# Layer 0 of an image network: the rows of cumulated steps from one transpose in place of four products with the triangle

## The chip, the core and the metric

The kernel runs on one core of a Trainium2 chip. The metric is the device time of one execution in microseconds (us); the number given for a kernel is the median of several runs. The engines are named as in the profile: PE is TensorE (matrix products), PEld its weight loads, DVE VectorE, ACT ScalarE, POOL GpSimd, SP SyncE, which here issues the DMAs.

## The reference, cut to what matters

Eight images of 64x64 pixels with 192 channels go through two layers. Layer 0 is, for each image: a group normalization, a 3x3 depthwise convolution, a layer norm, an input projection, a causal convolution of four taps, a state-space mixer (SSD) with 6 heads of 64 channels and 64 states, a gate and an RMS norm, an output projection, another 3x3 convolution, a layer norm and an MLP. Layer 1 is a selective scan in four directions. The change touches only the mixer of layer 0. What it computes there:

```python
dt = softplus(zxbcdt[..., DIN + CONVDIM:] + dt_bias)      # a step for each token and head
dA = dt * A                                               # A = -exp(A_log), one for each head
dA_cs = cumsum(dA, axis=2)                                # cumulated inside a chunk of tokens
seg = dA_cs[:, :, :, None, :] - dA_cs[:, :, None, :, :]   # token i minus token j, for each head
scores = einsum('bcin,bcjn->bcij', Cm, Bm)[..., None] * exp(seg) * dt[:, :, None, :, :]   # where j <= i
y = einsum('bcijh,bcjhp->bcihp', scores, x)
decay_last = exp(dA_cs[:, :, -1:, :] - dA_cs)
```

For `seg` the cumulated steps are needed twice: with the tokens along the partitions (as columns, one number for each partition), and with the tokens along the free axis (as rows), repeated on every partition.

## The kernel before, in words

Layer 0 (`layer0`) works on 64 tiles: 8 images times 8 tiles of 512 tokens (TT), each tile in 4 chunks (NQ) of 128 tokens (Q). The work of a tile is written as some eighteen chains (`statistics`, `inputs`, `conv1`, `norm1`, `gate`, `mix`, `convolve`, `steps_in_time`, `decays`, `powers`, `scores`, `turn`, `states`, `mixer`, `output`, `conv2`, `norm2`, `mlp`), each a generator that runs over all tiles and yields steps. Chains of different tiles overlap.

The order of the work on each engine is set by a planner, `Flow`. A step names its engine, an estimated duration (in us), and the instructions to issue. The planner keeps a clock for each engine; it takes again and again the step that can begin earliest (with a small rank for each chain as a tie-break), issues its instructions, and moves the clocks. `yield "take", tag` takes a buffer from a small pool ("mm": five PSUM banks of 512 columns; "sm": three; "csr": one), `f.give` returns it with its time, and `f.at[...]` notes when a result is due, for the chains that wait for it. An ACT step may name a table; where it differs from the current one, the planner counts a table load. The order that comes out is the order in which each engine works through its queue on the chip; the engines meet by semaphores only. So an estimate that is changed can move any later step on any engine.

The steps around the change, with their lines:

- `gate` (L531) makes p_z: the gate and the raw steps dr of a tile. L547 (DVE) adds the bias to dr.
- `steps_in_time` makes dt (ACT L566 to L568, DVE L577) and da = dt x A (DVE L578, 128 tokens x 4 chunks x 6 heads), then on PE three products with da (L588): with a strictly lower triangle, with an upper triangle `up` (1 where column >= row), and with ones. They go to p_c, 24 columns each. The middle 24 columns are the cumulated steps as columns; DVE copies them to cst (L594). ACT takes the exponential of all 72 columns (dec, L601), and DVE makes w2 from it (L607).
- `rows_of`, forked from there, makes the same cumulated steps as rows: for each chunk one product of da (128 tokens x 6 heads, the weights) with `up` (128 x 128, streamed), into p_cs, 6 rows x 512 columns (L617). ACT copies them to csr (L622), and SP stores csr in a scratch tensor csd in HBM (L625), [6, 512].
- `decays` loads from csd, for each chunk, the six rows of 128 numbers onto all 128 partitions: e (L640), 128 x 6 x 128.
- `powers` (ACT L653, L658) makes exp(-(relu(cs_i - e))) in e; its bias is a column of cst. `scores` multiplies e with the masked product p_g (L673, L677, L682), and `mixer` uses e as the weights of p_y (L790), after the skip products (L787).
- Other steps that are named below: p_x (L448, input projection), p_t and xdt, xw (L699, L705, L710: transposes of x and their weighting), p_b and bt (L715, L720), p_i and p_n (L740, L751, states), p_u and yc (L850, L859), p_o (L873), p_f (L956 and L976, the two halves of the MLP), the convolution steps xs and x on DVE (L343), and the sums s on POOL (L365).

Layer 1 begins after layer 0 has ended, and works with other functions.

Of the kernel before, what the change touches and what calls it, by code (L numbers as in the profile page):

```python
# [8 lines left out]
F32 = mybir.dt.float32  # L9
# [8 lines left out]
TT = 512  # L18
RT = TT // WI
NT = L // TT  # L20
Q = 128
NQ = TT // Q
NH, HD, NS = 6, 64, 64
# [30 lines left out]
def bc(ap, axis, shape):  # L54

    return ap.unsqueeze(axis).to_broadcast(shape)
# [37 lines left out]
class Flow:  # L94
# [24 lines left out]
    def pool(self, tag, n):  # L119
        self.slots[tag] = [0.0] * n  # L120
# [64 lines left out]
def step(engine, weight, do, after=None, table=None):  # L185
    return engine, weight, do, after, table


def layer0(tc, consts, x, x1s, mv1, w_in, w_out, w_fc1, w_fc2, rows):
    nc = tc.nc  # L190
    ident, low, up, grp, eps, ones96, ones1, p96, p128 = consts
# [10 lines left out]
    with ExitStack() as ctx:  # L202
# [6 lines left out]
        sp = pool("s0", 2)  # L209
        xxp = pool("xx0", 3)  # L210
        mp = pool("mm0", 5, space=PSUM)
        dsp = pool("cs0", 3, space=DRAM)
# [11 lines left out]
        ps = mp.tile([128, TT], F32, name="p_fb", tag="mm")  # L224
        for mt in range(6):
            for ct in range(CT):
# [4 lines left out]
                    start=ct == 0,  # L231
                    stop=ct == 1,
# [22 lines left out]
        f = Flow(tc)  # L255
# [4 lines left out]
        got = {}  # L260
# [294 lines left out]
        def steps_in_time():  # L555

            for T in range(len(tiles)):
                yield "wait", ("dr", T)
                dr = got["dr", T]
                dt = got["dt", T] = sp.tile([128, NQ, NH], F32, name="dt")  # L560
                da = got["da", T] = sp.tile([128, NQ, NH], F32, name="da")
                yield step(
                    "ACT",
                    0.8,
                    lambda: [
                        nc.scalar.activation(dt, dr, AF.Abs),  # L566
                        nc.scalar.activation(dt, dt, AF.Exp, scale=-1.0),
                        nc.scalar.activation(dt, dt, AF.Ln, bias=1.0),  # L568
                    ],
                    None,  # L570
                    "explog",
                )
                yield step(
                    "DVE",
                    0.4,
                    lambda: [
                        nc.vector.scalar_tensor_tensor(dt, dr, 0.0, dt, ALU.max, ALU.add),  # L577
                        nc.vector.tensor_mul(da, dt, bc(an, 1, [128, NQ, NH])),  # L578
                    ],
                )  # L580
                daf = da.rearrange("p a b -> p (a b)")
                yield "take", "sm"
                pc = qp.tile([128, DIN], F32, name="p_c", tag="sm")
                r = yield step(
                    "PE",
                    0.8,
                    lambda: [
                        nc.tensor.matmul(pc[:, i * 24 : i * 24 + 24], m, daf, start=True, stop=True)  # L588
                        for i, m in enumerate((low, up, ones1))
                    ],  # L590
                )
                cst = got["cst", T] = sp.tile([128, NQ, NH], F32, name="cst")
                yield step(
                    "DVE", 0.16, lambda: [nc.vector.tensor_copy(cst.rearrange("p a b -> p (a b)"), pc[:, 24:48])], r  # L594
                )
                f.fork(rows_of(T, da))
                dec = got["dec", T] = sp.tile([128, 3, NQ, NH], F32, name="dec")
                r = yield step(
                    "ACT",
                    0.3,  # L600
                    lambda: [nc.scalar.activation(dec.rearrange("p a b c -> p (a b c)"), pc[:, 0:72], AF.Exp)],  # L601
                    r,
                    "explog",
                )
                f.give("sm", r)
                w2 = got["w2", T] = sp.tile([128, NQ, NH], F32, name="w2")
                f.at["w2", T] = yield step("DVE", 0.2, lambda: [nc.vector.tensor_mul(w2, dt, dec[:, 0])])  # L607

        def rows_of(T, da):

            yield "take", "mm"
            ps = mp.tile([128, TT], F32, name="p_cs", tag="mm")
            r = yield step(
                "PE",
                1.0,
                lambda: [
                    nc.tensor.matmul(ps[:NH, c * Q : c * Q + Q], da[:, c], up, start=True, stop=True) for c in range(NQ)  # L617
                ],
            )
            yield "take", "csr"  # L620
            csr = sp.tile([NH, TT], F32, name="csr", bufs=1)
            r = yield step("ACT", 0.6, lambda: [nc.scalar.copy(csr, ps[:NH])], r)  # L622
            f.give("mm", r)
            csd = got["csd", T] = dsp.tile([NH, TT], F32, name="csd")
            r = yield step("SP", 0.1, lambda: [nc.sync.dma_start(out=csd, in_=csr)], r)  # L625
            f.give("csr", r + 2)
            f.at["cs", T] = r + 2.5
# [4 lines left out]
        def decays():  # L632

            for T in range(len(tiles)):
                yield "wait", ("cs", T)
                for c in range(NQ):
                    yield "take", "e"
                    e = got["e", T, c] = ch.tile([128, NH, Q], F32, name="e", bufs=5)
                    src = got["csd", T][:, c * Q : c * Q + Q].partition_broadcast(128)
                    r = yield step("SP", 0.1, lambda: [nc.sync.dma_start(out=e, in_=src)], f.at["cs", T])  # L640
                    f.at["csb", T, c] = r + 3

# [366 lines left out]
        for gen, rank in (  # L1009
            (mlp, -0.177),  # L1010
            (norm2, -0.056),
            (conv2, -0.275),
            (output, -0.03),
            (mixer, -0.08),
            (states, -0.04),
            (turn, -0.06),
            (scores, 0.017),
            (powers, -0.284),
            (decays, -0.195),
            (steps_in_time, 0.209),  # L1020
            (convolve, 0.071),
            (mix, -0.12),
            (gate, -0.17),
            (norm1, -0.14),
            (conv1, -0.254),
            (inputs, -0.313),
            (statistics, -0.298),
        ):
            f.chain(gen(), rank)
# [864 lines left out]
```

## Time and profile before

| | |
|---|---|
| median of 3 runs | 23751.5 us (23744.67 to 23764.05) |
| the profiled execution: its own time | 23759.13 us |
| its span, from first to last instruction | 23757.4 us |
| layer 0 in it (end of the last MLP product) | 0 to 4868 us |
| granted TensorE clock, mean | 0.972 |
| p_cs L617, 64 tiles x 4 products | 512 matmul instructions |
| csr<-p_cs L622, ACT | 64 x 575 ns (median) |
| cst<-p_c L594, DVE | 64 x 172 ns (median) |
| csd<-csr L625, SP issue | 64 x 283 ns (median) |
| e<-csd L640, SP issue, 384 KB each | 256 x 494 ns (median) |
| ACT_TABLE_LOAD in layer 0 | 356, 456.7 us |

An f32 product is recorded as two matmul instructions, a transpose as one. Matmuls are pipelined, so their recorded durations overlap. PEclk is the share of full clock that TensorE was granted. A row of who waited for whom names the waiter, the releaser, the total in us, how often, and the longest wait. The chain of waits is followed back from the last instruction: at each step to what released it, or to the instruction before it on its engine.

### The profile page before, as it was taken

How to read it: one execution, taken by the hardware profiler on the slowest of the kernel's cores; microseconds unless marked ns; L12 is line 12 of the kernel's file. 1: busy time of each engine (PE TensorE's matmuls, PEld its weight loads, DVE VectorE, ACT ScalarE, POOL GpSimd, SP SyncE). 2: the span in 40 equal slices, each digit the busy share in tenths (PEclk: the TensorE clock that was granted, in tenths of full speed). 3: DMA queues.
4: the chain of work that ended last, by engine and by line, in shares of the span. 5: the costliest groups of instructions: out<-in, count | busy, mean ns of one | idle time of the engine just before them, and what ended most of it. 6: DMA issues, size and time to landing. Idle time of an engine off the chain costs nothing.

```text
span 23757.4 us, 313126 instructions
## 1 busy us (share of the span) xinstructions
PE 21089.6 (89%) x100804; PEld 10279.5 (43%) x100804; DVE 21274.2 (90%) x22093; ACT 21040.0 (89%) x37507; POOL 16067.4 (68%) x12871
## 2 busy tenths in 40 slices
PE   7999999978888888888888888888888888888888
PEld 4444444434444444444444444444444444444444
DVE  7888888779998999899989998999899989998998
ACT  5666766669998999899989998999899989998998
POOL 1111111149995999599959985998699769976997
PEclk8999999989999999999999999999999999999999
DMA  2111111133233323333233233323332233233332
GB/s 50 45 44 44 46 44 43 39 99 81 81 79 107 81 82 78 107 81 82 76 112 81 82 77 109 81 81 79 110 82 81 78 107 82 81 85 100 82 83 67
DMA packets 1368290, 1859.75 MB, mean 78 GB/s; under 512 B 268576, under 2 KB 697024, under 8 KB 1357440
## 3 DMA queue, kind: packets, MB, share of 16 engines
q1 hardware_dynamic: 1366656, 1839.73, 28.7%
q8 instruction: 810, 13.27, 0.2%
q14 instruction: 824, 6.75, 0.1%
HBM read 1225.98 MB, written 210.50 MB: 60 GB/s over the span
## 4 chain that ended last, share of the span: by engine, by line
POOL 43%; PE 24%; ACT 15%; DVE 7%; issue 6%; DMA 4%; SPq 1%; POOLq 0%; ACTq 0%; DVEq 0%
POOL hc L1648 40%; ACT pw L1592 6%; ACT ea L1607 6%; POOL cy L1646 3%; PE p_f L956 3%; DMA xc<-xo 2%; DVE xs L1202 2%; PE p_f L976 2%; PE p_x L448 2%; PE y L1663 2%; PE p_o L873 2%; PE p_y L790 1%; PE g L1618 1%; PE p_d L1481 1%; PE p_z L531 1%
## 5 line engine op out<-in xcount | busy, mean ns | idle before, releaser
L1648 POOL TENSOR_TENSOR hc<-hs,cb 128x1024 f32<-128x1024 f32 x6144 | 14592.9, 2375 | 12.0 <-POOL cy L1646 9.9
L1634 DVE TENSOR_TENSOR_SCAN hs<-ea,cy,g 128x512 f32<-128x512 f32 x10752 | 13024.0, 1262 | 608.6 <-PE g L1618 411.1
L1592 ACT ACTIVATE pw<-duT,bt 128x384 f32<-128x384 f32 x16384 | 8874.1, 601 | 20.2 <-DVE duT L1539 20.2
L1607 ACT ACTIVATE ea<-dr,an 128x512 f32<-128x512 f32 x12288 | 8120.5, 709 | 189.2 <-DVE hs L1634 170.8
L1663 PE MATMUL y<-hc,sel 128*64 128x512 f32 x24576 | 6624.0, 617 | 1841.3 <-POOL hc L1648 1819.2
L1618 PEld LDWEIGHTS g<-ident,pw 128*128 128x128 f32 x49152 | 5288.7, 141 | 4336.8 <-issue 2671.4
L1618 PE MATMUL g<-ident,pw 128*128 128x128 f32 x49152 | 6788.4, 279 | 60.1 <-ACT pw L1592 28.6
L1646 POOL COPY cy<-hs 128x2 f32<-128x2 f32 x6144 | 1164.2, 189 | 3373.5 <-DMA out_x<-xl 1733.8
L1663 PEld LDWEIGHTS y<-hc,sel 128*64 128x64 f32 x24576 | 1225.9, 134 | 3254.1 <-POOL hc L1648 3031.3
L1634 DVE TENSOR_TENSOR_SCAN hs<-ea,g 128x512 f32<-128x512 f32 x1536 | 1763.7, 1202 | 159.0 <-PE g L1618 115.6
L365 POOL TENSOR_TENSOR s<-xs 96x512 f32<-96x512 f32 x64 | 121.1, 1892 | 2033.7 <-DVE xs L343 1522.9
L1202 DVE SCALAR_TENSOR_TENSOR xs<-pad,p,xs 128x4096 f32<-128x4096 f32 x192 | 860.9, 4484 | 43.4 <-ACT xs L1192 36.2
L1510 PE MATMUL p_dt<-xdbl,wd 13*128 13x512 f32 x1536 | 857.2, 639 | 41.0 <-DVE de L1523 39.1
L365 POOL TENSOR_TENSOR s<-sq 96x512 f32<-96x512 f32 x128 | 211.6, 1653 | 964.1 <-ACT sq L378 899.8
L1481 PE MATMUL p_d<-xc,wx 128*44 128x512 f32 x1536 | 791.6, 598 | 22.6 <-DMA xc<-xo 22.0
L343 DVE SCALAR_TENSOR_TENSOR x<-xx,p,x 96x512 f32<-96x512 f32 x1024 | 785.2, 815 | 19.4 <-ACT x L332 19.4
L956 PE MATMUL p_f<-h,wf 96*128 96x512 f32 x1536 | 761.9, 632 | 24.4 <-ACT zs L550 14.0
L343 DVE SCALAR_TENSOR_TENSOR xs<-xin,p,xs 96x512 f32<-96x512 f32 x1024 | 749.3, 767 | 4.6 <-ACT xs L332 4.6
L976 PE MATMUL p_f<-m,wf 128*96 128x512 f32 x1536 | 692.9, 601 | 0.0
L1532 PEld LDWEIGHTS p_du<-ident,de 128*128 128x128 f32 x3072 | 323.5, 141 | 610.2 <-DVE de L1523 405.8
L448 PE MATMUL p_x<-h,wi 96*128 96x512 f32 x1024 | 544.5, 664 | 12.3 <-ACT h L405 11.1
L365 POOL TENSOR_TENSOR s<-x 96x512 f32<-96x512 f32 x64 | 96.2, 1502 | 626.3 <-DVE x L343 477.2
(202 smaller groups left out, 19557.2 us busy)
## 6 DMA issues: line engine op xcount, KB each, us to landing
cb<-cd SPq DMA_DIRECT2D x4096, 128.0 KB
dr<-de SPq DMA_DIRECT2D x3072, 128.0 KB
xc<-xo SPq DMA_DIRECT2D x256, 768.0 KB
e<-csd SPq DMA_DIRECT2D x256, 384.0 KB
xl<-x SPq DMA_DIRECT2D x256, 384.0 KB
ut<-xo SPq DMA_DIRECT2D x128, 768.0 KB
ut<-xo SPq DMA_DIRECT2D x256, 384.0 KB
xo<-xs SPq DMA_DIRECT2D x48, 1024.0 KB
```

Of the source, the lines that this page charges most:

```text
L343: nc.vector.scalar_tensor_tensor(im(out[:, ct]), tap(ct, j), w[:, ct, j : j + 1], im(out[:, ct]), ALU.mult, ALU.add)
L956: nc.tensor.matmul(ps, wf1[:, ct, mt * 128 : mt * 128 + 128], h[:, ct], start=ct == 0, stop=ct == 1)
L976: nc.tensor.matmul(ps[:CP], wf2[:, kt, ct * CP : ct * CP + CP], m[:, kt], start=kt == 0, stop=kt == 5)
L1202: nc.vector.scalar_tensor_tensor(xs, tap(j), kw[:, d, j : j + 1], xs, ALU.mult, ALU.add)
L1481: nc.tensor.matmul(st["p_d"][:44], wx[:, d, k], st["xc"][:, d], start=d == 0, stop=d == DT - 1)
L1592: nc.scalar.activation(st["pw", p, j][:, :, i], st["duT"][:, j].rearrange("p (g c) -> p g c", c=64), AF.Copy, scale=st["bt"][:, j, n : n + 1],
L1607: nc.scalar.activation(ea[:, f], state[s]["dr", d][:, f], AF.Exp, scale=an[:, k, p, at : at + 1])
L1618: nc.tensor.transpose(g[:, f, j * 128 : j * 128 + 128], state[s]["pw", p, j][:, 2 * d + f].rearrange("p a b -> p (a b)"), ident,)
L1634: nc.vector.tensor_tensor_scan(rev(h[:, f]), rev(ea[:, f]), rev(g[:, f]), 0.0 if first(s) else state[s - 1]["cy"][:, p, d, f : f + 1], ALU ...
L1646: o(nc.gpsimd.tensor_copy(st["cy"][:, p, d], h[:, :, last]))
L1648: o(nc.gpsimd.tensor_mul(hc, h, bc(st["cb", p], 1, [128, 2, TT])))
L1663: o(nc.tensor.matmul(y[half[f]], sel, hc[:, f], start=p == 0 and k > 0, stop=p == NP1 - 1))
```

## The change

`rows_of` no longer multiplies da with the triangle. It takes cst, the cumulated steps as columns (128 tokens x 24: 4 chunks x 6 heads), and transposes it on PE: 24 rows x 128 columns, a row for each chunk and head. The copy csr, the scratch tensor csd and the loads of e follow the new layout: csr and csd are [24, 128], and chunk c's six rows lie at c x 6. The step on PE is now ready when cst is (q), and its estimate is 0.2 in place of 1.0; the estimate of ACT's copy is 0.3 in place of 0.6.

```diff
                 cst = got["cst", T] = sp.tile([128, NQ, NH], F32, name="cst")
-                yield step(
+                q = yield step(
                     "DVE", 0.16, lambda: [nc.vector.tensor_copy(cst.rearrange("p a b -> p (a b)"), pc[:, 24:48])], r
                 )
-                f.fork(rows_of(T, da))
+                f.fork(rows_of(T, cst, q))
...
-        def rows_of(T, da):
+        def rows_of(T, cst, r):
 
             yield "take", "mm"
             ps = mp.tile([128, TT], F32, name="p_cs", tag="mm")
             r = yield step(
                 "PE",
-                1.0,
-                lambda: [
-                    nc.tensor.matmul(ps[:NH, c * Q : c * Q + Q], da[:, c], up, start=True, stop=True) for c in range(NQ)
-                ],
+                0.2,
+                lambda: [nc.tensor.transpose(ps[: NQ * NH, :Q], cst.rearrange("p a b -> p (a b)"), ident)],
+                r,
             )
             yield "take", "csr"
-            csr = sp.tile([NH, TT], F32, name="csr", bufs=1)
-            r = yield step("ACT", 0.6, lambda: [nc.scalar.copy(csr, ps[:NH])], r)
+            csr = sp.tile([NQ * NH, Q], F32, name="csr", bufs=1)
+            r = yield step("ACT", 0.3, lambda: [nc.scalar.copy(csr, ps[: NQ * NH, :Q])], r)
             f.give("mm", r)
-            csd = got["csd", T] = dsp.tile([NH, TT], F32, name="csd")
+            csd = got["csd", T] = dsp.tile([NQ * NH, Q], F32, name="csd")
             r = yield step("SP", 0.1, lambda: [nc.sync.dma_start(out=csd, in_=csr)], r)
...
-                    src = got["csd", T][:, c * Q : c * Q + Q].partition_broadcast(128)
+                    src = got["csd", T][c * NH : c * NH + NH].partition_broadcast(128)
```

## The prediction

> **What bounds the kernel now.** I read the busy table in two stretches first, layer 0 (0 to 4868 us, where the last product of its MLP ends) and the rest, because every changed line stands in layer 0.
>
> ```profile
> core 0: us, PE busy (x) PEld busy (x) DVE busy (x) ACT busy (x) POOL busy (x), PEclk, DMA share, GB/s
> 0.00:4868.00 4868.00, 4496.60 (x15272) 2235.76 (x15272) 3899.60 (x6459) 3178.97 (x6133) 704.51 (x548) 0.92 0.18 44
> 4868.00:23757.00 18889.00, 16593.03 (x85533) 8043.76 (x85532) 17374.60 (x15634) 17861.01 (x31374) 15362.92 (x12323) 0.99 0.32 87
> ```
>
> In layer 0 PE is busy 92% of the time, DVE 80%, ACT 65%; the granted clock is 0.92. Next, who waits for whom between 100 and 4650 us (waiter, releaser, us in total, times, longest): PE's largest rows, then DVE's largest.
>
> ```profile
> PE p_c L588 <- DVE da L578: 42.6, 19, 4.8
> PE p_b L715 <- DVE xw L710: 27.2, 34, 2.4
> PE p_u L850 <- ACT yt L843: 24.7, 21, 4.4
> ...
> DVE xdt L705 <- PE p_y L790: 353.8, 142, 8.7
> ```
>
> PE's waits are small and spread; DVE waits for PE far more than PE for DVE. PE's idle time from 100 to 4750 us is 294 of 4650 us, 4.6 us for each of the 64 tiles. Then the chain of waits, asked in stretches of 150 us over layer 0: I added its pieces by engine and got PE 3792 us, DVE 800, ACT 197, DMA 57. So PE's in-order queue sets the pace, with DVE taking over for about a sixth. One stretch shows the products in question:
>
> ```profile
> 1574.90 1.11 PE p_c L588 x6
> 1576.01 1.47 PE p_n L751 x2
> 1577.48 3.71 PE p_f L956 x4
> 1581.19 1.80 PE p_cs L617 x8
> ```
>
> The columns are start, length, engine, tile and line, and how many instructions; x8 is four products of two instructions each.
>
> Last, the tile p_cs itself (min/median/max ns):
>
> ```profile
> L617 PEld LDWEIGHTS p_cs<-up,da x512: 83/88/136, 84.6 to 4662.7; 128*6 128x6 f32 x171
> L617 PE MATMUL p_cs<-up,da x512: 272/273/421, 84.6 to 4662.8; 128*6 128x128 f32 x171
> L622 ACT COPY csr<-p_cs x64: 558/575/577, 89.0 to 4663.6; 6x512 f32<-6x512 f32 x64
> ```
>
> Its 273 ns is not its cost, since products overlap. I therefore took each of the 64 groups in the trace from its first matmul's start to the start of the next group on PE: 41 of them take 0.97 us, 16 take 1.80, the others from 1.15 to 5.74; the mean is 1.33 and the sum 84.9 us. On the chain of waits lie 40 of the 64, with 49.4 us.
>
> **What the Trainium skill says.** "TensorE: Matmul & The Clock Gate", Part 4 (PE-mode transpose): about 275 ns for a 128x128 transpose in a kernel, output to PSUM, so that a copy must follow. The trace agrees in the duration (p_t at L699: median 273 ns), but in a stream three p_t take 0.33 us, so a step is 0.11 us. Same page, Part 1: the array runs at half clock after an idle window. The trace agrees: p_cs takes 0.97 or 1.80 us, nearly one to two. "ScalarE: Activation LUTs", "What ACT_TABLE_LOAD costs": about 1283 ns a load and 1380 ns of drain. Every load here takes 1283 ns; of the drain the stretch at 1575.64 us shows nothing, as dec follows at once. "DMA: Bandwidth & Descriptors", Specifications: full rate needs 512 B or more for each transfer. No shape, old or new, is below it, and no run so far shows the new ones.
>
> **The change part by part.**
>
> 1. The products. Removed per tile: 4 f32 products, 8 matmuls, 1.33 us on average. Added: one transpose with 24 columns as its weights and the identity streamed. Its nearest row is p_t: 256 groups of three last 0.50 us on average to the next group, waits included, so 0.17 us; alone at full clock 0.11. I take 0.17, 10.7 us for 64. So 84.9 - 10.7 = 74 us of PE's queue go. On the path lie 40 of the 64: 49.4 - 40 x 0.17 = 43 us. Between them stands the truth, because taking PE time away in a stretch where DVE leads still lets DVE's PE inputs come earlier. I take the middle, -58 (ends -43 and -74). With the work gone, DVE is next: 800 us of chain are its already.
>
> 2. The new wait. The transpose reads cst, which DVE copies out of p_c (L594), where the products read da, which p_c had already needed. In the trace the copy ends 0.22 to 3.21 us after p_c's last matmul, 0.97 on average, while p_cs begins 2.89 us after it on average. Set at the same places, the transpose would find cst missing in 11 tiles, 9.1 us in all. The built order has the transpose right behind p_c (nothing between) in 8 tiles, where it was 5 before, and at 3.2 products behind on average instead of 4.6. I take +12. The ends: 0, if it is always covered by the products between, and 64 x 0.97 = +62, if never. All of PE's queue stands behind it: p_x, p_g, p_t, p_n, and through them DVE's xdt and gm. A gain from this wait is excluded; it is only added.
>
> 3. ACT. The copy csr shrinks from 512 to 128 columns. bt (64 columns) takes 213 ns, yc (384) 479, so 0.83 ns a column and 0.27 us here, against 0.575: 64 x 0.31 = 20 us less. Beside this, the planner's new order needs fewer table loads: ahead of layer 1 the built order has 314 where it had 355, so 41 x 1.283 = 53 us less. ACT's chain share is 197 of 3179 us busy, 6%: 73 x 0.06 = 4.5 us. At most, PE's waits on ACT, about 93 us in the list, could shrink by a part; I take -10 (ends 0 and -40).
>
> 4. DMAs. csd is stored as 24 rows of 512 B, before 6 of 2 KB; each of the four e loads fetches one run of 3 KB per partition, before six of 512 B. The bytes stay (384 KB a load). On SP the store's issue takes 0.28 us, the e issues 250 us in all; the e issues may get shorter, and xin and xl, queued behind them on SP, would come no later. ACT waits for e 26 us in 21 places, and the order leaves 10 us or more of PE work between p_cs and the first p_y. I take 0 (ends +5, should 24 short rows be stored more slowly, and -15). The work that hides it is that 10 to 20 us of PE products; without it up to 26 us of ACT's waits would be at stake.
>
> 5. The order. The step is entered with 0.2 in place of 1.0 and the copy with 0.3 in place of 0.6, so the planner places everything after the first tile anew. I compared the built orders of PE: between p_y and p_u stand 11 us of products in the median before and 12 after, between p_t and p_n 12.6 and 11.8, between p_z and p_c 12.4 and 11.6 (counted with the stream times of the trace). None of these covers changes much. After the first images the new order repeats exactly each image, and the fc1 products of a tile stand closer together. I take 0, with both ends open: a fifth of PE's idle 294 us either way, 59 us. A longer PE pause also costs by the half clock after it, which is within that figure.
>
> Layer 1 keeps its order and shapes: 0.
>
> Sum: -58 + 12 - 10 + 0 + 0 = -56 us. Against the profiled execution, 23759.1 us (span 23757.4), that is 23703; the median of the runs shown is 7.6 us less, 23751.5, so 23695.
>
> **The rivals.**
>
> A, the forecast: PE's saving is passed on, 23695, by its own terms from 23655 to 23725. For it: PE at 92%, 40 of 64 groups on the chain.
>
> B, the new order is also better: A with a fifth less idle time, -56 - 59 = -115, 23636. For it: 41 table loads fewer, and a regular order. Against it: the covers above are about the same.
>
> C, the saving is hidden: only the 43 us on the path count, and the wait for cst takes their place at 0.97 us in those 40 tiles, 43 - 39 = 4, 23748. For it: DVE is at 80% and copies cst late where it is behind. Against it: in the old places only 11 tiles would wait.
>
> D, slower: the planner's new order makes PE stand longer in layer 0. The mechanism is one: an in-order PE queue meets inputs from DVE or ACT (da, xw, yt in the list above) that are not ready, and then runs at half clock. Each further us of idle time per tile costs 64 us; it decides from 56 us on, 0.9 us per tile over today's 4.6, and passes 0.2% at 1.6. I price it at 40% more idle time: 118 - 56 = +62, 23813. Against it: the covers hardly change.
>
> That the change doesn't do what it says is excluded by the built order: one transpose of 24x128 stands where four products stood.
>
> **How the numbers follow.** Chances: A 0.54, B 0.17, C 0.17, D 0.12. The likeliest is A: 23695. The range goes from B's middle part to C's end, 23620 to 23760; outside are the far half of B (0.07) and D (0.12). A measurement can tell about 0.2%, 47.5 us, from no change. Of A I count 0.36 as faster by more than that and 0.18 within. Faster 0.36 + 0.17 = 0.53, within 0.18 + 0.17 = 0.35, slower 0.12.
>
> **What would show it.** Right: one p_cs matmul per tile with 0.11 to 0.2 us to the next, csr at about 0.27 us, 41 table loads fewer, PE's idle time in layer 0 near 294 us, layer 1 still 18889 us long, and the last fc2 product near 4812 us. Wrong in step 2: a row "PE p_cs <- DVE cst" of over 30 us. Wrong in step 5: PE's idle time off by over 60 us, or a granted clock away from 0.92. Wrong in step 4: DMA waits of e above 26 us. If the span of layer 1 moves by over 20 us, the whole argument misses a place.

## The result, and the profile after

| | before | after |
|---|---|---|
| median, 15 runs each | 23751.5 us (23738.77 to 23777.2) | 23708.01 us (23688.35 to 23722.78) |
| ratio, 95% interval | | 0.998 (0.9972 to 0.9987) |
| span of the profiled execution | 23757.4 us | 23706.3 us |
| layer 0 in it | 4868.0 us | 4806.6 us |
| the rest of it | 18889.4 us | 18899.7 us |

The changed kernel is 43.5 us faster, with an interval from 31 to 66 us. The forecast was 56 us, 23695.

First the busy table in the two stretches, layer 0 and the rest, of the changed kernel:

```profile
core 0: us, PE busy (x) PEld busy (x) DVE busy (x) ACT busy (x) POOL busy (x), PEclk, DMA share, GB/s
0.00:4807.00 4807.00, 4412.07 (x14824) 2178.96 (x14824) 3880.74 (x6460) 3102.15 (x6093) 649.17 (x550) 0.93 0.16 44
4807.00:23706.00 18899.00, 16600.51 (x85532) 8054.40 (x85532) 17376.49 (x15634) 17859.55 (x31374) 15351.88 (x12322) 0.98 0.32 87
```

The 448 matmuls that are gone (512 of the products, less 64 transposes) leave PE 85 us less busy in layer 0; ACT is 77 us less busy. PE's idle time in layer 0, end less busy, grew from 371.4 to 394.5 us. The rest has the same counts as before but for one record on POOL and on PE, and took 10 us longer in this execution.

Then the tile p_cs, with what waited:

```profile
L616 PEld LDWEIGHTS p_cs<-ident,cst x64: 90/93/143, 85.9 to 4605.7; 128*24 128x24 f32 x64
L616 PE MATMUL p_cs<-ident,cst x64: 269/275/422, 85.9 to 4605.7; 128*24 128x128 f32 x64
L621 ACT COPY csr<-p_cs x64: 237/254/256, 86.4 to 4606.0; 24x128 f32<-24x128 f32 x64
```

A transpose records 275 ns, as one matmul of the old products did (273), and there are an eighth as many. Taken as in the prediction, from the group's first matmul to the start of the next group on PE, 39 of the 64 take 0.11 or 0.12 us; the mean is 0.26 and the sum 16.6 us, with waits, against 84.9. The copy takes 254 ns in place of 575. In the chain of waits a transpose looks like this:

```profile
1472.88 0.58 PE p_c L588 x6
1473.47 0.84 PE p_i L739 x2
1474.31 1.92 PE p_f L955 x4
1476.22 0.11 PE p_cs L616
1476.33 0.79 PE p_n L750 x2
```

Over layer 0, added up in the same stretches of 150 us, the chain now has PE 3483 us (3792 before), DVE 1065 (800), ACT 206 (197), DMA 74 (57). The step p_cs still lies on it 38 times, but with 6.6 us in place of 49.4. DVE has gained 265 us of the chain, as point 1 of the prediction named it, and PE still leads.

Last, PE's waits between 100 and 4600 us:

```profile
PE p_f L955 <- ACT zs L550: 27.4, 21, 2.2
PE p_c L588 <- DVE da L578: 23.4, 19, 4.8
...
PE p_g L672 <- DVE t L741: 17.3, 6, 3.9
PE p_b L714 <- DVE xw L709: 16.6, 23, 1.2
PE p_n L750 <- DVE yt L802: 13.1, 12, 1.6
PE p_cs L616 <- ACT zs L550: 10.0, 6, 2.2
```

In the kernel before, PE's row for zs was this:

```profile
PE p_f L956 <- ACT zs L550: 14.0, 10, 4.1
```

Some waits shrank (p_c for da 42.6 to 23.4, p_b for xw 27.2 to 16.6), others grew or are new (p_f for zs 14.0 to 27.4, p_g for t, and p_cs for a bank that ACT's zs has to free). Such a reshuffle is the mark of a new order on all engines, not of one new wait. So the 43 us may come from the PE time, from the new order, or from both.

### The profile page after: what moved, and what is told of

Same layout as the page of the kernel before. It is cut to its first block, busy times and chain, and to the rows that moved or that the text cites. A ratio compares the mean times of both kernels' runs of the same rounds, so it can differ in the third digit from the quotient of the medians.

```text
span 23706.3 us, 312102 instructions
## 1 busy us (share of the span) xinstructions
PE 21012.6 (89%) x100356; PEld 10233.4 (43%) x100356; DVE 21257.2 (90%) x22093; ACT 20961.7 (88%) x37466; POOL 16001.1 (67%) x12871
## 4 chain that ended last, share of the span: by engine, by line
POOL 46%; PE 22%; ACT 13%; DVE 8%; issue 6%; DMA 3%; SPq 1%; POOLq 0%; ACTq 0%; DVEq 0%
POOL hc L1647 43%; ACT pw L1591 5%; ACT ea L1606 5%; POOL cy L1645 3%; PE p_f L955 3%; DVE xs L1201 2%; DMA xc<-xo 2%; PE p_x L448 2%; PE p_f L975 2%; PE y L1662 2%; PE p_o L872 1%; PE g L1617 1%; PE p_y L789 1%; PE p_d L1480 1%; PE p_z L531 1%
## 5 line engine op out<-in xcount | busy, mean ns | idle before, releaser
L1480 PE MATMUL p_d<-xc,wx 128*44 128x512 f32 x1536 | 788.7, 596 | 23.4 <-DMA xc<-xo 23.4
L955 PE MATMUL p_f<-h,wf 96*128 96x512 f32 x1536 | 757.2, 631 | 43.8 <-ACT zs L550 27.4
```

Of the source, the lines that this page charges most:

```text
L955: nc.tensor.matmul(ps, wf1[:, ct, mt * 128 : mt * 128 + 128], h[:, ct], start=ct == 0, stop=ct == 1)
```

## The experiments

The change can be cut in two: the work (transpose, short copy, new layout) and the order (the estimates and the ready time that the planner is given). The first four runs tell them apart in the full kernel, and ran beside one another; before was 23757.96 us there (64 runs).

### The products in the new order

Edit to the kernel before: the products stay, the planner's input changes.

```diff
-                f.fork(rows_of(T, da))
+                f.fork(rows_of(T, da, q))
...
-                1.0,
+                0.2,
...
-            r = yield step("ACT", 0.6, lambda: [nc.scalar.copy(csr, ps[:NH])], r)
+            r = yield step("ACT", 0.3, lambda: [nc.scalar.copy(csr, ps[:NH])], r)
```

(q is cst's time, and the PE step gets it as its ready time.)

> The four products with the triangle stay, with csr, csd and e as before, but the planner gets the new estimates (0.2 and 0.3) and the new ready time, so that every engine's queue stands in the order of the changed kernel. Theory 1 (the gain is PE time taken off the path, the order is worth little): between -15 and +25 us against before, layer 0 near 4868 us. Theory 2 (the gain is the new order with its 41 table loads fewer): about -43 us, as much as the whole change. Theory 3 (the order costs a part of a larger gain): +15 to +40 us, PE idle in layer 0 about 20 us over before's 371.

Measured: 23787.94 us, +30.0; ratio 1.0012 (1.0006 to 1.0019). In its profile, layer 0:

```profile
0.00:4880.00 4880.00, 4495.26 (x15272) 2217.70 (x15272) 3886.41 (x6459) 3126.03 (x6092) 651.10 (x548) 0.93 0.18 44
```

ACT is 53 us less busy than before, as 41 table loads fewer would have it, and layer 0 is still 12 us longer. So the new order alone, and its loads with it, gain nothing while the products stay: theory 2 falls. Theory 3's range for this run (+15 to +40) holds.

### The transpose in the old order

Edit to the changed kernel: 1.0 for 0.2, 0.6 for 0.3, and no ready time on the PE step, so that the queues stand as before.

> The transpose, the short copy and the new layout, but the planner gets the old estimates (1.0 and 0.6) and the old ready time, so that the queues stand in the order of the kernel before. Theory 1: -43 to -74 us against before (the removed products, 84.9 us on PE, less the transposes). Theory 2: within 15 us of before. Theory 3: more than the change as a whole, -60 to -75 us, because the old order gives nothing back. A row of PE waiting for cst of about 9 us, or up to 39 if the wait eats the saving.

Measured: 23751.57 us, -6.4; ratio 0.9998 (0.9989 to 1.0006), no change that can be told. Theory 1, in the form that the removed PE time is passed on whatever the order, falls too, and so does theory 3, which asked for -60 to -75 here. Theory 2's range for this run holds, but not the one for the run before: none of the three fits both. Its layer 0, and the wait on cst:

```profile
0.00:4836.00 4836.00, 4446.45 (x14824) 2206.37 (x14824) 3902.56 (x6459) 3159.00 (x6133) 701.74 (x548) 0.92 0.16 44
```

```profile
PE p_n L749 <- DVE gm L675: 13.7, 11, 5.0
...
PE p_cs L616 <- DVE cst L594: 7.5, 9, 1.8
```

The wait on cst is 7.5 us, near the 9.1 that the trace of before gave for these places. In this execution layer 0 was 32 us shorter than before's, though not by the 65 us that left the p_cs stream (each group from its start to the next, less the wait ahead of the next: 78.0 to 12.6 us). Found again are 17 us in the stream time of fc2 (667.4 to 684.3, its last tile left out) at the same count of products, 9.5 in fc1 and 18.5 us in waits (368.9 to 387.4); the input projection p_x gave some 11 us more.

### The old layout in HBM

```diff
-            csd = got["csd", T] = dsp.tile([NQ * NH, Q], F32, name="csd")
-            r = yield step("SP", 0.1, lambda: [nc.sync.dma_start(out=csd, in_=csr)], r)
+            csd = got["csd", T] = dsp.tile([NH, TT], F32, name="csd")
+            dst = csd.rearrange("h (c q) -> c h q", c=NQ)
+            r = yield step("SP", 0.1, lambda: [nc.sync.dma_start(out=dst, in_=csr)], r)
...
-                    src = got["csd", T][c * NH : c * NH + NH].partition_broadcast(128)
+                    src = got["csd", T][:, c * Q : c * Q + Q].partition_broadcast(128)
```

> The changed kernel with the scratch tensor in the old layout: the store writes its 24 rows of 512 B into [6, 512], each load of e fetches six pieces of 512 B per partition in place of one of 3 KB. All queues keep the order of the changed kernel. If the layout is worth nothing on the path: the time of the changed kernel within 10 us, about -43 against before. If the longer pieces are part of the gain: 15 to 30 us slower than the changed kernel, with ACT's wait for e grown from 31 us to over 50.

Measured: 23723.28 us, -34.7 against before; ratio 0.9986 (0.9979 to 0.9993), an interval that overlaps the changed kernel's. The tile e, in the changed kernel and then in this one:

```profile
L639 SPq DMA_DIRECT2D e<-csd x256: 319/382/2114, 89.1 to 4609.0; - x128
...
  DMA e<-csd: 31.1, 16
```

```profile
L640 SPq DMA_DIRECT2D e<-csd x256: 360/535/2989, 89.3 to 4618.0; - x128
...
  DMA e<-csd: 65.9, 38
```

The longer pieces do what was thought of them: issuing is shorter (115 us in all 256, against 265 here) and ACT waits 31 us in place of 66. By the medians, each against its own before, 9 us of that reach the end; the intervals allow nothing, and also more than 9.

### The products twice

```diff
-                    nc.tensor.matmul(ps[:NH, c * Q : c * Q + Q], da[:, c], up, start=True, stop=True) for c in range(NQ)
+                    nc.tensor.matmul(ps[:NH, c * Q : c * Q + Q], da[:, c], up, start=True, stop=True)
+                    for _ in range(2)
+                    for c in range(NQ)
```

> The kernel before with each of the four products issued twice to the same place, the estimates unchanged, so the same order with 64 more groups of about 1.0 to 1.3 us on PE. Theory 1, with the middle of the path share (58 of 74): +50 to +67 us against before. If all PE time counts: +65 to +85. If only groups on the chain count (40 of 64): +40 to +50. If PE's time is hidden: under +20.

Measured: 23784.95 us, +27.0; ratio 1.0013 (1.0006 to 1.002). Its layer 0:

```profile
0.00:4897.00 4897.00, 4541.21 (x15784) 2277.88 (x15784) 3895.65 (x6459) 3180.30 (x6133) 700.09 (x548) 0.92 0.18 43
```

There are 512 matmuls more, and in the trace the p_cs groups grew from 84.9 to 146.8 us, by 62. So 0.44 of the added PE time reaches the end. That lies in none of the ranges set beforehand: it is between "hidden" (under 20) and the 40 to 50 us of "only on the chain".

### Layer 0 alone

Layer 1 spans 18886 to 18913 us in the traces though its work is the same, a spread of more than half the effect. So four kernels without layer 1 ran beside one another, four or five executions each:

```diff
-    x1s = [dp.tile([C, L], F32, name=f"x1_{b}") for b in range(nb)]
+    x1s = [out[b] for b in range(nb)]
...
-    layer1(tc, (ident, grp, eps, p128), x1s, mv1, out, w_in1, w_x, w_dt, w_out1)
```

> Layer 1 is left out; layer 0 of the kernel before writes its result straight to the output, all layer 0 queues in their old order. Every theory: 4870 to 4890 us, layer 0's 4868 us of the full trace and the end of the last store. It is the base for the three that run beside it.

> Layer 1 is left out; layer 0 of the changed kernel. Theory 1 (all of the change lies in layer 0, and what the full runs show less is spread of layer 1): 55 to 65 us less than layer 0 of before alone, as the one trace had it (61). Theory 2 (layer 0 gains only the 43 us that the medians of the full kernel show, and the one trace was a lucky one): 35 to 48 us less.

> Layer 1 is left out; the four products in the order of the changed kernel. If the order and the work add up (additive theory): the sum of this difference to before and that of the transpose in the old order is the difference of the changed kernel. If they work together: this one 5 to 25 us slower than before, although the order with the transposes is faster than the old order with the transposes.

> Layer 1 is left out; the transpose in the order of the kernel before. Additive theory: 60 us and more less than before, if the order costs 12 (as one trace of the products in the new order has it). Theory of the order that hides: 25 to 38 us less than before, as one trace has it, so half of the PE time taken away is found again as waiting and slow clock. If the median of the full kernel (6 us less) is true of layer 0: 0 to 12 us less.

| layer 0 alone | old order | new order |
|---|---|---|
| products | 4854.87 us (4844.92 to 4863.86) | 4919.96 us (4886.73 to 4934.63) |
| transpose | 4850.26 us (4842.74 to 4857.39) | 4820.27 us (4804.85 to 4823.29) |

In sign the pattern of the full kernels comes back; the products in the new order lose 65 us here, and lost 30 in the full kernel. The kernel before came out under its range (4870 to 4890), and the products in the new order over theirs (5 to 25 us slower). The changed kernel gains 35 us, as the second of its two theories had it, which suggests that the 61 us of its one trace were in part a lucky pair of executions. The work is worth 5 us in the old order and 100 in the new; the order costs 65 us with the products and gains 30 with the transpose. They work together, and no sum of two terms holds. The two cells that gain nothing are those where the estimate given to the planner is not the duration of what runs: 1.0 for a transpose, 0.2 for the products. (The ready time and the copy's estimate go with the order in all four; neither was tried by itself. The cells with the products keep the old layout in HBM too.) Two theories remain: an estimate that fits gives a good order, or each new order is a draw in a lottery and these were two blanks.

Within each kernel the longer executions show the lower granted clock, to within 0.001: the products in the new order took 4887 us at 0.927 and 4935 at 0.918. The spread inside a cell goes with the clock. Between the kernels it isn't the clock alone: at 0.920 stand one execution of 4922 us with the products in the new order and, from the runs of the next section, one of 4813 with the transpose at 0.3.

### Other estimates that fit

Layer 1 is left out again; one number is changed in each: the estimate of the transpose to 0.16 and to 0.3, that of the products to 1.2. Even these small steps put some 1900 to 2800 of the 3400 groups of products on PE in other places, so they are new draws, if it is a lottery.

> Layer 1 is left out; the changed kernel with 0.16 in place of 0.2 as the planner's estimate of the transpose, which is as near to its measured 0.11 to 0.26 us. Nothing else changes, but about half of PE's queue comes to stand in other places, and the order has 339 table loads in place of 315. Theory of the fitting estimate (an estimate near the real duration gives a good order): 4805 to 4835 us, as with 0.2 (4820). Theory of the lottery (each new order moves the time by tens of us in either way): anywhere from 4790 to 4880, unlike 4820 by more than 15 us. If table loads count: 24 x 1.28 = 31 us of ACT, 2 to 15 us slower.

> Layer 1 is left out; the changed kernel with 0.3 in place of 0.2 as the estimate of the transpose, 343 table loads. Theory of the fitting estimate: 4805 to 4840 us, since 0.3 is still near. Theory of the lottery: anywhere from 4790 to 4880, and unlike the run with 0.16.

> Layer 1 is left out; the kernel before with 1.2 in place of 1.0 as the estimate of the four products, which took 1.33 us on average, so it fits at least as well; 315 table loads in place of 356. Theory of the fitting estimate: 4835 to 4870 us, as with 1.0 (4855) or a little better. Theory of the lottery: anywhere from 4830 to 4930, unlike 4855 by more than 15 us. If table loads count: 10 us and more faster than 4855.

The full kernel before took 23760.19 us beside these and 23743.74 beside the four above, 0.07% apart, which is 3 us of layer 0.

Measured: the transpose at 0.16 4810.4 us (4781.08 to 4823.52), at 0.3 4810.23 us (4804.17 to 4813.31); the products at 1.2 4839.1 us (4824.69 to 4845.2). With the first draws, the transpose with a fitting estimate is at 4820, 4810 and 4810, mean 4814; the products at 4855 and 4839, mean 4847. The lottery among fitting estimates is worth 10 to 16 us, less than the 33 us between the two means, and the misfits stand at 4850 and 4920, each above all its fitting kin by 30 us or more. That speaks for the fitting estimate, though seven kernels don't prove it. Not every mark was on its side: the products at 1.2 differ from those at 1.0 by 15.8 us, which meets the mark of the lottery (more than 15), and with 315 loads in place of 356 they are more than 10 us faster, which meets that of the table loads. Elsewhere the loads don't show: 339 and 343 with the two fastest, 315 with 4820, and 315 with 4920 too.

### The full kernel at 0.3

> The full changed kernel with 0.3 in place of 0.2 as the estimate of the transpose, since layer 0 alone was 10 us faster with it (4810 against 4820) and its runs lay closer together. If that carries over to the full kernel: -45 to -60 us against before, at or a little below the changed kernel's -43. If the 10 us are spread between chips: -30 to -45.

Measured: 23703.64 us against 23760.51 beside it, -56.9; ratio 0.9977 (0.9968 to 0.9985). It is the fastest full kernel measured, but its interval covers the changed kernel's 0.998, so it isn't shown to be faster than that.

With its trace, layer 0 of the full kernels can be split into PE's busy and idle time, one execution each:

| layer 0, in us | length | PE busy | PE idle | granted clock |
|---|---|---|---|---|
| before | 4868.0 | 4496.6 | 371.4 | 0.921 |
| products, new order | 4880.5 | 4495.8 | 384.7 | 0.925 |
| transpose, old order | 4836.3 | 4446.8 | 389.5 | 0.919 |
| changed kernel | 4806.6 | 4412.1 | 394.5 | 0.929 |
| transpose at 0.3 | 4808.3 | 4436.3 | 372.0 | 0.918 |

The last three issue the same 14824 matmuls. The changed kernel is 30 us shorter than the transpose in the old order although PE waits no less in it: the same matmuls took less time, at a higher granted clock. The kernel at 0.3 is as short at the lowest clock, because PE waits some 20 us less. (In the trace of before, the 41 groups p_cs of 0.97 us lie at full granted clock and the 16 of 1.80 us at half.) So the fitting orders were good in two different ways, and what a fitting estimate does to the order isn't shown.

## Why the prediction was right, and where its steps were off

The sign, the stage and the size held: -43.5 us for -56. That they held is in part luck. The wait (+12) and ACT (-10) cancelled in the sum, and neither was found at its size. And the order, put at 0, decided whether the saving arrived: with the same work in the old order 6.4 us came through, which is rival C's result. The band given to A, 23655 to 23725, isn't the sum of the ends of its terms either; without the order's, they reach from 23622 to 23775. Point by point:

1. The products. The queue lost 68 us (84.9 less 16.6), near the 74 of the sum, and DVE is next on the chain, as said. The term that was mis-sized is what is passed on: "the middle, -58". Orders that fit give 33 us in layer 0 alone, half of the 68, with the small terms in it; doubling the products gives 0.44. The full kernels give more, 0.64 for the changed one and 0.81 at 0.3, and the old order gives 0.1. So the share isn't a constant of the stage. In the changed kernel's trace some of what is freed on PE becomes wait (the idle time rose by 23 us); at 0.3 none does.

2. The wait. +12 was too much for the changed kernel. PE waits for cst 2.8 us in 3 places by the row of the tile cst. In the old order it was 7.5. What stands ahead of p_cs is instead a bank, 10.0 us for ACT's zs in 6 places, a wait that the prediction did not name. It comes with the order: in layer 0 alone the products in the new order meet it with 10.0 us too.

3. ACT. The copy is 0.32 us shorter, the loads are 41 fewer: 77 us less ACT time, 73 forecast. The -10 that it was to bring isn't seen by itself: with the same 315 loads, the products in layer 0 alone took 4920 us in one order and 4839 in another. As a cause of the gain the loads aren't shown.

4. DMAs. Forecast 0; the old layout in the new order cost 9 us with overlapping intervals. The issues became shorter, as thought. The mark against this step, DMA waits of e above 26 us, did come: they are 31.1 us in 16 places in the changed kernel, and before they were these:

```profile
  DMA e<-csd: 26.0, 21
```

With the new layout in the old order they were 10.8, and with the old layout in the new order 65.9. So the layout didn't lengthen them; the order did.

5. The order, "0, with both ends open". The covers compared there did not tell what it would do. The order is worth between -37 us (with the transpose: -43.5 less -6.4) and +30 (with the products). It wasn't a separate term: the estimate belongs to the work. Rival C, the hidden saving, is what came about where the order was held (6 us less), but in the trace by slower fc1 and fc2 products and small waits, and only for 7.5 us by the wait on cst that it named. Rival D's mechanism, longer waits from a new order, is seen in small where the products kept their length under an estimate of 0.2: PE's idle time is 13 us longer there. Rival B did not come: PE's idle time did not fall.

Of the marks set for being right most came: 59 of the 64 transposes take 0.11 to 0.21 us to the next group, the copy csr 0.254 us, and the last fc2 product ends at 4806.6 us for 4812. PE's idle time, 294 us between 100 and 4750 us before, is 326 there, off by less than the 60 that would have counted as wrong.

What stays open is why so little of the saving arrives in the old order. Its traces show layer 0 21 to 32 us shorter than before's, and the medians 5 or 6, because one trace is one draw: in layer 0 alone the profiled execution was the fastest of its four (4842.74) and before's was the slowest of its four (4863.86), and in the full kernel's trace layer 1 was 24 us longer than before's. In layer 0 alone this kernel has a granted clock of 0.916 to 0.919, below before's 0.922 to 0.927. That fits a saving lost to a slower PE, but no run takes the clock apart from the order.

## What to carry to other kernels

Where a planner writes the order, a change of work and its estimate are one change: measure them together, and test the estimate alone before the order is credited or blamed. Here PE was 92% busy with DVE at 80%, and between 0.1 and 0.8 of the time taken away from PE reached the end, by order; that is this kernel's figure and no rule. Cross the work with the order, two by two, before telling where a gain of a few tens of us comes from. An execution or two can't: here one trace said 61 us and the medians 43.

## What was not expected of the hardware

The same layer 1 took 18886 to 18913 us in the traces of the full kernels, with equal counts of instructions. A product's stream time moves with what stands around it: fc2's matmuls (1512, without the last tile) took 667.4 us in the order of before and 684.3 in the same order with the transposes. A lower granted clock fits that (0.921 and 0.919 over layer 0 of the two traces), but no run took it apart. And a load of the same 384 KB was issued in 0.38 us with pieces of 3 KB and 0.54 us with pieces of 512 B (medians).
